# Borders between the stages of a two-layer sparse graph attention kernel: smaller units at two ends, an earlier mean row, buffers kept for the last stage

## The chip, the cores and the metric

The kernel runs on one core of one Trainium2 chip. The metric is the device time of that core in microseconds (us), lower is better. The time shown for the kernel before is the median of three runs. A profiled execution of the same kernel is shown beside it; all durations of single instructions come from that one.

## What is computed

Two graph attention layers over 4096 nodes with 512 features each. `adj` is a 4096 x 4096 matrix of 0 and 1, in which row n has few ones (its neighbours) except for the first rows. Cut to what matters:

```python
def _L0_gnn_ref(node_matrix, adj, W, a):          # 8 heads of 64
    h = einsum('nf,kfp->knp', node_matrix, W)
    e = leaky_relu(f2[:, :, None] + f1[:, None, :], 0.2)   # f1, f2: h times the halves of a
    att = softmax(where(adj[None] > 0, e, NEG_INF))
    return einsum('knm,kmp->knp', att, h)         # heads side by side: 512 features

def _L1_gnn_ref(x, adj, W1, a1, Wo, ao, lin1_w, lin1_b, lin2_w, lin2_b):
    x1 = elu(gat_heads(x, adj > 0, W1, a1))       # 8 heads of 64
    out = elu(gat_heads(x1, adj > 0, Wo, ao))     # 1 head of 512
    out = relu(out @ lin1_w + lin1_b)             # 1024 wide
    return out @ lin2_w + lin2_b

x = layernorm(x + _L0_gnn_ref(x, adj, ...))
x = layernorm(x + _L1_gnn_ref(x, adj, ...))
```

A node without neighbours gets, by the softmax over equal values, the mean of all rows of h. All arithmetic is in float32.

## The kernel before

There are three attention steps, called t0 (layer 0), t1 (the first attention of layer 1) and t2 (its second attention, with the two dense products behind it). In the text they are "layer 0", "layer 1" and "the last stage". Ahead of them one stage reads `adj` in 32 tiles of 128 rows and turns it into lists of edges (`find_edges`), with the projection for t0 beside it.

**Tables and gathers.** For each step a table in DRAM (`table_t0`, `table_t1`, `table_t2`) holds one row per node: its projected features and one or two scores. Row 4096, the last, is the mean of all rows; nodes without neighbours point at it. The edges of a tile of 128 nodes lie in chunks of 128 edges. One indirect DMA (line 1076), issued on the GpSimd queue (POOL), fetches the 128 table rows of a chunk into a slot of a buffer `g` with room for 6 chunks. A gather waits for every write to its table, the mean row among them.

**Units.** A tile's chunks are handled in units of up to 6 chunks (`units_of`). Each has two groups of slots, for the first and the second 64 nodes of the tile. There are 309 chunks and 66 units in each step. For every unit the loop runs, in this order on the engines:

- `weights` of the *next* unit: scores of the edges on VectorE (DVE, lines 1147 to 1150), their exponentials on ScalarE (ACT, lines 1152 to 1158). They wait for that unit's gathers.
- `add` of this unit: DVE writes selection matrices `sm` (line 1179, or 1187 in the last stage) and, in the two layers, scales the gathered rows (line 1200); TensorE (PE) sums them into `acc` (line 1212), 64 output rows at a time.
- the gather of the unit that takes over this unit's buffer: 7 ahead in the layers (`GB = 7`), 4 ahead in the last stage (`GT = 4`).

Between them stand the steps of a finished tile (`divide`, `norm`, `project`, `rows`, `split`), which make the next step's table: transposes (line 683), projection (line 697), the row `hrow` and its DMA to the table (line 711), and for every eight tiles `split_s`, five DVE instructions (lines 723 to 733) that cut the scores s into three bfloat16 parts. `spread` (lines 1101 to 1129) brings these scores to the edges of a tile with matmuls and two or more DVE instructions.

**The end of a layer.** Tile 0 is the last one, and has most edges; its last unit has 5 chunks, 5 slots in the first group and 1 in the second. In front of the last unit's `add`, `mean_of_all_but` makes the mean row's first part, out of all tiles but the last one (four DVE instructions, 16 matmuls and two ACT copies). When the last tile has been projected, `split` runs, then `rows`, and after everything `finish_mean` adds the last tile's part (lines 768 and 769) and sends the mean row (line 770). In the last round the split of s, which the DVE runs in order, comes ahead of the adds of `finish_mean`.

**The last stage.** At the end of the layers their memory is released. The last stage takes 4 buffers `g` of its own (pool `tg`), clears them on POOL (line 1428, four memsets), gathers for the first four units, and loads the weights of the dense products on the SyncE queue (SP): `sl1w` and `sl2w`, 2 MB each, then the biases. Buffers are cleared once because a slot that stands for no edge is not written by its gather, and what lies there must be a finite number. Layer 0 clears its 7 buffers the same way, on ACT (line 1288); layer 1 uses them on. The bias of the first dense product is loaded as 8 rows (`sl1b_r`) and turned with one transpose (line 1507) ahead of the first unit. Dense products are called in pieces between units (lines 1479 and 1491), at a pace set by the number of chunks.

All orders inside the layers and the last stage are written out by hand (`tc.manual_schedule()`); waits follow from the tiles and their pools. Where a pool lies in memory decides for whom its first writer waits: with `reuse_waits="tile"` a new tile waits for the last users of the tiles that lay at its place.

Of the kernel before, what the change touches and what calls it, by code (L numbers as in the profile page):

```python
# [10 lines left out]
F32 = mybir.dt.float32  # L11
# [10 lines left out]
P = 128  # L22
N = 4096
F = 512
NT = N // P
# [7 lines left out]
HC = HID // P  # L33
# [4 lines left out]
HS = 8  # L38
DM = 64
HN = P // 2  # L40
GC = 6
GB = 7
# [3 lines left out]
GT = 4  # L46
# [512 lines left out]
def sparse_path(  # L559
# [23 lines left out]
    nc = tc.nc  # L583
# [15 lines left out]
    ident = const.tile([P, P], F32, name="s_ident")  # L599
# [40 lines left out]
    st2 = Stage2("t2", 1, 512, dest_first=True)  # L640
# [391 lines left out]
    class Unit:  # L1032
# [3 lines left out]
        def __init__(self, t, runs, slots):  # L1036
# [2 lines left out]
            self.n = len(self.chunks)  # L1039
            self.first = self.last = False  # L1040

        def pick(self, a, base=0):

            at = 0
            for first, n in self.runs:
                yield slice(at, at + n), a[:, first - base : first - base + n]
                at += n
# [17 lines left out]
    class Attention:  # L1065
# [5 lines left out]

        def gather(self, u):

            u.g = self.gp.tile([P, GC, F + HS], F32, name="g")
            for k, c in enumerate(u.chunks):
                nc.gpsimd.indirect_dma_start(  # L1076
                    out=u.g[:, k, : self.st.row],
                    out_offset=None,
                    in_=self.st.table[:, :],
                    in_offset=bass.IndirectOffsetOnAxis(ap=idx[:, c : c + 1], axis=0),  # L1080
                    bounds_check=N,
                    oob_is_err=False,
                )
# [76 lines left out]
        def add(self, u):  # L1160

            hs, n = self.st.heads, u.n
# [8 lines left out]
            todo, at = [], 0  # L1171
            for g, slots in enumerate(u.slots):
                of_g = iota_n[:, g * HN : (g + 1) * HN]
                if hs > 1:
                    k, n_ = slots[0], len(slots)
                    c = u.chunks[k]
                    assert u.chunks[k : k + n_] == list(range(c, c + n_))
                    shape = [P, n_, HN]
                    nc.vector.tensor_tensor(  # L1179
                        sm[:, at : at + n_],  # L1180
                        of_g[:, None, :].to_broadcast(shape),
                        nl[:, c : c + n_, None].to_broadcast(shape),
                        op=OP.is_equal,
                    )
# [85 lines left out]
    def heads_layer(gp, wk, sb, pp, st, nxt, fetch, finish, clear):  # L1270
# [5 lines left out]
        order = [t for pair in zip(range(NT - 1, NT // 2, -1), many) for t in pair] + [NT // 2, 0]  # L1276
        assert sorted(order) == list(range(NT))
        units = units_of(order)
        with tc.tile_pool(name=f"ha_{st.name}", bufs=2, space=PSUM, reuse_waits="tile") as pacc, \
                tc.tile_pool(name=f"hp_{st.name}", bufs=1, space=PSUM, reuse_waits="tile") as one, \  # L1280
                tc.tile_pool(name=f"hq_{st.name}", bufs=2, space=PSUM, reuse_waits="tile") as ps, \
# [2 lines left out]
            extra = {}  # L1284
            if clear:
                for _ in range(GB):
                    g = gp.tile([P, GC * (F + HS)], F32, name="g")
                    nc.scalar.activation(g, ones.to_broadcast(g.shape), AF.Copy, scale=0.0)
            for u in units[:GB]:
                at.gather(u)  # L1290
# [38 lines left out]
            for i, u in enumerate(units):  # L1329
# [5 lines left out]
                run(project)  # L1335
                if i + 1 < len(units):
                    at.weights(units[i + 1])
                if i == len(units) - 1:
                    mrow = mean_of_all_but(pp, ps, nxt, u.t)
                at.add(u)  # L1340
                if i + GB < len(units):
# [8 lines left out]
                    spread()  # L1350
            ways.append((divide, order[-1]))
            while ways:
                for of in (project, split, rows, norm, divide):
                    run(of)
            finish_mean(ps, nxt, mrow)


    layers = ctx.enter_context(ExitStack())
# [24 lines left out]
        project_mean(sb, pp, st0)  # L1383


    wk = ctx.enter_context(tc.tile_pool(name="lw", bufs=3, reuse_waits="tile"))
    sb = ctx.enter_context(tc.tile_pool(name="ls", bufs=2, reuse_waits="tile"))
    pp = layers.enter_context(tc.tile_pool(name="lp", bufs=2, side="right", reuse_waits="tile"))
    gp = layers.enter_context(tc.tile_pool(name="lg", bufs=GB, side="right", reuse_waits="tile"))

    def fetch0(t):
        xr = sb.tile([P, F], F32, name="xr", bufs=3)
# [15 lines left out]


    layers.close()  # L1410
    with tc.tile_pool(name="tg", bufs=GT, side="right", reuse_waits="tile") as gp, \
            tc.tile_pool(name="tb", bufs=1, side="right", reuse_waits="tile") as big, \
            tc.tile_pool(name="ta", bufs=2, space=PSUM, reuse_waits="tile") as pacc, \
            tc.tile_pool(name="tp", bufs=1, space=PSUM, reuse_waits="tile") as ps, tc.manual_schedule():

# [7 lines left out]
        assert sorted(sum(blocks, [])) == list(range(NT))  # L1423
        order = [t for block in blocks for t in block]
        units = units_of(order)
        at = Attention(st2, gp, wk, pacc, ps)
        for _ in range(GT):
            nc.gpsimd.memset(gp.tile([P, GC, F + HS], F32, name="g"), 0.0)
        for u in units[:GT]:
            at.gather(u)  # L1430
        l1w = big.tile([P, FC, HID], F32, name="sl1w")
        nc.sync.dma_start(l1w, lin1_w.rearrange("(c p) o -> p c o", p=P))
        l2w = big.tile([P, HC, F], F32, name="sl2w")
        nc.sync.dma_start(l2w, lin2_w.rearrange("(c p) o -> p c o", p=P))
        l1b_r = big.tile([HC, P], F32, name="sl1b_r")
        nc.sync.dma_start(l1b_r, lin1_b.rearrange("(c p) -> c p", p=P))
        l2b = big.tile([P, F], F32, name="sl2b")
        nc.sync.dma_start(l2b, lin2_b.partition_broadcast(P))
        hts, hids, ready, open_ = {}, {}, [], []
# [63 lines left out]
            at.spread(t)()  # L1503
        at.weights(units[0])
        l1b = big.tile([P, HC], F32, name="sl1b")
        pb = ps.tile([P, HC], F32, name="pt")
        nc.tensor.transpose(pb, l1b_r, ident[:HC, :HC])
        nc.vector.tensor_copy(l1b, pb)


        pace = {t: 0.0 for t in blocks[0]}
# [2 lines left out]
            pace.update((t, 2 * len(last) / chunks) for t in block)  # L1514
        due, folded = 0.0, None
        for i, u in enumerate(units):
            pos = order.index(u.t)
            spread = at.spread(order[pos + 2]) if u.first and pos + 2 < NT else None
            if folded:
# [81 lines left out]
```

## Time and profile before

| | us |
|---|---|
| time before, median of 3 runs | 2330.81 (2325.15 to 2334.34) |
| profiled execution | 2138.83 |
| its span, first to last instruction | 2136.3 |
| PE busy in the span | 1721.8 (81%) |
| DVE busy | 1328.6 (62%) |
| POOL busy | 1162.0 (54%) |
| ACT busy | 663.4 (31%) |
| mean granted PE clock of the profiled execution | 0.918 |

The profiled execution is 9% shorter than the runs without a profile; sums are made against its own time. Layer 0 begins to gather at 500.5 us, layer 1 at 944.1 us and the last stage at 1384.2 us. A line of the timeline gives start and duration in us, engine, line of the kernel, operation, what it writes and reads, how many were merged, and in brackets the idle time before it with what ended it.

### The profile page before, as it was taken

Reading aid. Unit: us, or ns where it says so; the run is one execution under the profiler, and the core shown is the slowest. Engines: PE = TensorE matmul, PEld = TensorE weight load, DVE = VectorE, ACT = ScalarE, POOL = GpSimd, SP = SyncE. Lnnn points to the kernel's source line nnn. Section 1 sums busy time; section 2 is a strip of 40 time slices with the busy share of each in tenths; the row PEclk is TensorE's granted clock in tenths of the full one; section 3 lists DMA queues with packets and bytes.
Section 4 is the critical chain, followed back from the end, with each engine's and each line's share of the span. In section 5 each row is a group of like instructions: output and inputs, shape, how many; then the busy total and the mean of one; then the engine's idle time right before and its main releaser. Section 6 shows DMA issues by size and latency. Waiting matters only on the chain.

```text
span 2136.3 us, 29277 instructions
## 1 busy us (share of the span) xinstructions
PE 1721.8 (81%) x8987; PEld 1004.8 (47%) x8987; DVE 1328.6 (62%) x3920; ACT 663.4 (31%) x2311; POOL 1162.0 (54%) x1662
## 2 busy tenths in 40 slices
PE   4878777663798888857887888569999998998997
PEld 3655443221465565534555655344444444444444
DVE  5787777774889998837878878433434343433413
ACT  3346777664222232102333332111110212111121
POOL 5514444346777777727777777473547443543200
PEclk8999998786999999878999999889999999999999
DMA  6434566544777878727767776463546343534301
GB/s 229 132 109 168 188 250 238 201 153 130 228 233 231 248 242 243 208 67 191 196 185 195 195 198 190 151 165 102 156 119 177 113 128 96 148 103 120 96 19 46
DMA packets 132589, 351.94 MB, mean 165 GB/s; under 512 B 41922, under 2 KB 42954, under 8 KB 128454
## 3 DMA queue, kind: packets, MB, share of 16 engines
q0 software_dynamic: 74160, 206.25, 35.4%
q1 hardware_dynamic: 58262, 143.72, 19.1%
q8 instruction: 74, 1.21, 0.2%
q14 instruction: 93, 0.76, 0.1%
HBM read 347.31 MB, written 42.24 MB: 182 GB/s over the span
## 4 chain that ended last, share of the span: by engine, by line
PE 33%; DVE 17%; issue 16%; POOL 15%; DMA 12%; ACT 6%; SPq 0%; POOLq 0%; DVEq 0%; ACTq 0%
POOL g L1076 10%; DMA g<-table_t,idx 10%; PE acc L1212 10%; PE p L1479 9%; PE ph L697 6%; DVE g L1200 4%; PE p L1491 4%; DVE cand L884 2%; POOL s L944 1%; ACT sides L943 1%; DMA xr<-sx_d 1%; DVE cand L901 1%; DVE sm L1179 1%; DVE lst L899 1%; PE pl L967 1%
## 5 line engine op out<-in xcount | busy, mean ns | idle before, releaser
L1076 POOL DMA_INDIRECT g<-table_t,idx x927 | 937.8, 1012 | 535.9 <-issue 229.1
L1212 PE MATMUL acc<-g,sm 128*64 128x260 f32 (+2 forms) x4068 | 581.0, 416 | 182.7 <-DVE g L1200 141.6
L1212 PEld LDWEIGHTS acc<-g,sm 128*64 128x64 f32 x4068 | 327.9, 148 | 402.1 <-DVE g L1200 159.5
L697 PE MATMUL ph<-sw_t,xt 128*128 128x264 f32 (+1 forms) x1536 | 399.5, 409 | 54.3 <-ACT xt L686 47.8
L697 PEld LDWEIGHTS ph<-sw_t,xt 128*128 128x128 f32 x1536 | 296.5, 199 | 126.3 <-ACT xt L686 70.6
L1200 DVE TENSOR_TENSOR g<-g,wp 128x2048 f32<-128x2048 f32 (+3 forms) x132 | 348.9, 2644 | 3.4 <-ACT wp L1155 3.4
L884 DVE MAX8 cand<-key 128x8 f32<-128x353 f32 (+55 forms) x467 | 196.3, 446 | 77.6 <-PE key L878 76.8
L1479 PE MATMUL p<-sht,sl1w 128*128 128x512 f32 (+1 forms) x576 | 228.9, 553 | 0.5 <-DVE xr L1496 0.5
L1491 PE MATMUL p<-sl2w,shid 128*128 128x512 f32 x512 | 226.7, 597 | 0.0
L686 ACT ACTIVATE xt<-pt 128x128 f32<-128x128 f32 x384 | 101.1, 278 | 214.3 <-PE pt L683 213.9
L1479 PEld LDWEIGHTS p<-sht,sl1w 128*128 128x128 f32 x576 | 108.0, 191 | 111.6 <-issue 106.0
L1491 PEld LDWEIGHTS p<-sl2w,shid 128*128 128x128 f32 x512 | 95.2, 190 | 119.8 <-issue 119.4
L1147 DVE TENSOR_TENSOR z<-s,g 128x16 f32<-128x16 f32 (+8 forms) x291 | 46.6, 175 | 162.7 <-DMA g<-table_t,idx 161.6
L877 PE MATMUL key<-sg,s_identb 128*128 128x512 bf16 (+1 forms) x258 | 111.5, 433 | 14.3 <-DVE cand L884 9.0
L1482 ACT ACTIVATE shid<-p,sl1b 128x512 f32<-128x512 f32 (+1 forms) x72 | 46.0, 639 | 242.8 <-PE p L1479 242.8
L1249 DVE SCALAR_TENSOR_TENSOR o<-ex,o 128x512 f32<-128x512 f32 x64 | 44.2, 691 | 122.0 <-ACT ex L1248 121.8
L848 ACT ACTIVATE sg<-raw 128x4096 bf16<-128x4096 int32 (+1 forms) x39 | 116.9, 2998 | 6.3 <-DMA raw<-in_adj_dram 3.4
L710 ACT COPY hrow<-ph 128x260 f32<-128x260 f32 (+2 forms) x194 | 70.5, 372 | 152.3 <-PE ph L697 152.0
L878 PE MATMUL key<-frac,places 128*128 128x512 bf16 (+1 forms) x258 | 111.4, 433 | 2.7 <-POOL places L784 2.7
L1187 DVE TENSOR_SCALAR sm<-iota_n,nl,w 128x64 f32<-128x64 f32 x339 | 83.6, 327 | 31.2 <-ACT w L1158 31.2
L1155 ACT ACTIVATE wp<-z 128x32 f32<-128x32 f32 (+3 forms) x132 | 27.2, 206 | 211.2 <-DVE g L1200 211.2
L1496 DVE TENSOR_TENSOR xr<-p,xr 128x512 f32<-128x512 f32 x32 | 22.0, 689 | 93.6 <-PE p L1491 93.2
(185 smaller groups left out, 1853.5 us busy)
## 6 DMA issues: line engine op xcount, KB each, us to landing
raw<-in_adj_dram SPq DMA_DIRECT2D x31, 2048.0 KB, 7.7
table_t<-hrow SPq DMA_DIRECT2D x64, 260.0 KB, 3.2
xr<-in_x_dram SPq DMA_DIRECT2D x64, 256.0 KB, 3.9
g<-table_t,idx POOLq DMA_INDIRECT x927, 3.8
table_t<-hrow SPq DMA_DIRECT2D x32, 257.0 KB, 4.4
sx_d<-o SPq DMA_DIRECT2D x32, 256.0 KB, 4.0
xr<-sx_d SPq DMA_DIRECT2D x32, 256.0 KB, 4.4
out_dram<-xr SPq DMA_DIRECT2D x32, 256.0 KB, 2.3
```

Source lines behind the costliest of these rows:

```text
L686: nc.scalar.activation(xt[:, c, :], pt[:, c, :], AF.Copy, accum_out=st.xparts[:, c, t : t + 1])
L697: nc.tensor.matmul(ph[:n], columns(c), st.w[:, c, j], start=(c == 0), stop=(c == FC - 1))
L848: nc.scalar.activation(sg[:, ts(i, w)], raw[:, ts(i, w)], AF.Sign)
L877: nc.tensor.matmul(out_, ident_b, sg[:, j:e], start=True, stop=False)
L878: nc.tensor.matmul(out_, places[:, w], frac[:, j - w * KW : e - w * KW], start=False, stop=True)
L884: nc.vector.max(out=cand[:, at : at + 8], in_=part)
L1076: nc.gpsimd.indirect_dma_start(out=u.g[:, k, : self.st.row], out_offset=None, in_=self.st.table[:, :], in_offset=bass.IndirectOffsetOnAxis ...
L1187: nc.vector.tensor_scalar(sm[:, at + i], of_g, node[k], u.w[:, k], op0=OP.is_equal, op1=OP.mult)
L1200: nc.vector.tensor_mul(body, body, wp[:, :, :, None].to_broadcast(body.shape))
L1212: nc.tensor.matmul(out_[g * HN : (g + 1) * HN], sm[:, slot], rows(k), start=start, stop=stop)
L1479: nc.tensor.matmul(p1, l1w[:, c, ts(k, P)], hts[b][:, c, :n], start=(c == 0), stop=(c == FC - 1))
L1491: nc.tensor.matmul(p2, hids[b][:, k, ts(j, P)], l2w[:, k, :], start=(k == 0), stop=(k == HC - 1))
```

## The change

Four edits:

1. The last unit of each layer is cut in two: all chunks but the last two, and the last two (`Unit.cut`). The first unit of the last stage is cut into its first two chunks and the rest.
2. `mean_of_all_but` is called one unit of tile 0 earlier (two units ahead of the last, counted with the cut).
3. In the last rounds of a layer `rows` runs ahead of `split`, and `finish_mean` directly behind the last `rows`.
4. Four of the layers' seven buffers `g` lie in a pool `lk` that is kept; the last stage goes on with these four and doesn't clear any. The four memsets on POOL go. Buffers are handed out by a counter: turns 0 to 3 of every 7 from the kept pool, 4 to 6 from the pool `lg`, which ends with the layers. In the last stage `sl1b_r` is loaded ahead of the weights, and its transpose and copy come at the third unit.

```diff
+        def cut(self, m):
+            (first, n), = self.runs
+            one = Unit(self.t, [(first, m)], [[k for k in slots if k < m] for slots in self.slots])
+            two = Unit(self.t, [(first + m, n - m)], [[k - m for k in slots if k >= m] for slots in self.slots])
+            one.first, two.last = self.first, self.last
+            return [one, two]
...
-            u.g = self.gp.tile([P, GC, F + HS], F32, name="g")
+            u.g = self.gp()
...
-                if hs > 1:
+                if hs > 1 and slots:
...
         units = units_of(order)
+        units[-1:] = units[-1].cut(units[-1].n - 2)
...
-                    g = gp.tile([P, GC * (F + HS)], F32, name="g")
+                    g = gp().rearrange("p k f -> p (k f)")
                     nc.scalar.activation(g, ones.to_broadcast(g.shape), AF.Copy, scale=0.0)
...
-                if i == len(units) - 1:
+                if i == len(units) - 3:
                     mrow = mean_of_all_but(pp, ps, nxt, u.t)
...
             while ways:
-                for of in (project, split, rows, norm, divide):
+                for of in (project, rows, split, norm, divide):
                     run(of)
-            finish_mean(ps, nxt, mrow)
+                    if of is rows and len(out_) == NT:
+                        finish_mean(ps, nxt, mrow)
...
+    keep = ctx.enter_context(tc.tile_pool(name="lk", bufs=GT, reuse_waits="tile"))
     wk = ctx.enter_context(tc.tile_pool(name="lw", bufs=3, reuse_waits="tile"))
...
-    gp = layers.enter_context(tc.tile_pool(name="lg", bufs=GB, side="right", reuse_waits="tile"))
+    more = layers.enter_context(tc.tile_pool(name="lg", bufs=GB - GT, side="right", reuse_waits="tile"))
+    turns = [0]
+    def gp():
+        turns[0] += 1
+        return (keep if (turns[0] - 1) % GB < GT else more).tile([P, GC, F + HS], F32, name="g")
...
-    with tc.tile_pool(name="tg", bufs=GT, side="right", reuse_waits="tile") as gp, \
-            tc.tile_pool(name="tb", bufs=1, side="right", reuse_waits="tile") as big, \
+    with tc.tile_pool(name="tb", bufs=1, side="right", reuse_waits="tile") as big, \
...
-        at = Attention(st2, gp, wk, pacc, ps)
-        for _ in range(GT):
-            nc.gpsimd.memset(gp.tile([P, GC, F + HS], F32, name="g"), 0.0)
+        units[:1] = units[0].cut(2)
+        at = Attention(st2, lambda: keep.tile([P, GC, F + HS], F32, name="g"), wk, pacc, ps)
         for u in units[:GT]:
             at.gather(u)
+        l1b_r = big.tile([HC, P], F32, name="sl1b_r")
+        nc.sync.dma_start(l1b_r, lin1_b.rearrange("(c p) -> c p", p=P))
         l1w = big.tile([P, FC, HID], F32, name="sl1w")
...
-        l1b_r = big.tile([HC, P], F32, name="sl1b_r")
-        nc.sync.dma_start(l1b_r, lin1_b.rearrange("(c p) -> c p", p=P))
...
-        pb = ps.tile([P, HC], F32, name="pt")
-        nc.tensor.transpose(pb, l1b_r, ident[:HC, :HC])
-        nc.vector.tensor_copy(l1b, pb)
...
         for i, u in enumerate(units):
+            if i == 2:
+                pb = ps.tile([P, HC], F32, name="pt")
+                nc.tensor.transpose(pb, l1b_r, ident[:HC, :HC])
+                nc.vector.tensor_copy(l1b, pb)
             pos = order.index(u.t)
```

## The prediction

> **What bounds the kernel now.** I read the page's chain of waits first, then the windows of the stretch between layer 1 and the last stage, then its timeline, because every edit sits at a border between stages: the end of layer 0 (near 920 us), the end of layer 1 (near 1360 us), the start of the last stage (near 1384 us).
>
> ```profile
> PE 33%; DVE 17%; issue 16%; POOL 15%; DMA 12%; ACT 6%; SPq 0%; POOLq 0%; DVEq 0%; ACTq 0%
> ...
> 1370.00:1380.00 10.00, 5.13 (x29) 3.27 (x27) 4.05 (x11) 0.81 (x3) 4.04 (x2) 0.84 0.12 43
> 1380.00:1390.00 10.00, 0.00 (x0) 0.00 (x0) 0.00 (x0) 0.00 (x0) 8.62 (x7) 0.50 0.37 105
> 1390.00:1400.00 10.00, 0.00 (x0) 0.00 (x0) 0.87 (x6) 0.21 (x1) 7.56 (x9) 0.50 0.64 179
> ...
> 1440.00:1450.00 10.00, 10.00 (x65) 7.76 (x64) 3.56 (x15) 3.73 (x8) 7.56 (x9) 1.00 0.73 194
> ```
>
> No one engine owns the chain, so a change pays only where its stage waits. The windows (length, then busy PE, weight load, DVE, ACT, POOL, then clock, DMA share, GB/s) show such a place: from 1380 to 1400 TensorE does nothing, and from about 1427 it is full. The timeline says why.
>
> ```profile
> 1350.34 2.70 POOL L1428 MEMSET g<- 128x3120 f32 x1 [1.35 <-PE acc L1212]
> ...
> 1373.26 2.70 POOL L1428 MEMSET g<- 128x3120 f32 x1 [20.22 <-PE ph L697]
> ...
> 1373.66 1.03 PE L768 MATMUL ph<-hrow,s_share 128*1 128x256 f32 x4 [0.46 <-ACT ss_t L717]
> ...
> 1373.92 2.07 DVE L730 CAST s_t<-s 128x16 bf16<-128x16 f32 x1
> ...
> 1376.56 0.73 DVE L769 TENSOR_TENSOR mrow<-mrow,ph 1x256 f32<-1x256 f32 x2
> ...
> 1377.32 0.25 SPq L770 DMA_DIRECT2D table_t<-mrow  x1
> ...
> 1378.65 5.34 POOL L1428 MEMSET g<- 128x3120 f32 x2 [2.70 <-DMA table_t<-mrow]
> ...
> 1384.15 1.00 POOL L1076 DMA_INDIRECT g<-table_t,idx  x1 [0.16 <-POOL g L1428]
> ...
> 1422.57 0.17 DVE L1147 TENSOR_TENSOR z<-s,g 128x6 f32<-128x6 f32 x1 [3.43 <-DMA g<-table_t,idx]
> ...
> 1423.68 3.35 PE L1212 MATMUL acc<-g,sm 128*64 128x257 f32 x24 [2.85 <-DVE sm L1187]
> ...
> 1426.97 7.17 PE L1479 MATMUL p<-sht,sl1w 128*128 128x256 f32 x32
> ```
>
> The reader is to see one chain: the last row of the table is projected, the mean row's second part waits on DVE behind the split of s (whose CAST takes 2.07 us, while the same CAST took 0.18 at 1321.94), the mean row is sent at 1377.32, two memsets follow on POOL, and only then the first gather goes at 1384.15. After that the gathers pace everything, one per 1.3 us on POOL, until the 27th chunk: it lands by 1422.57, lets the sums of the tile before it start at 1423.68, and from 1426.97, the first dense product, TensorE has no gap. So what counts is when chunk 27 lands. Last, the tail of both layers:
>
> ```profile
> 910.65 8.45 PE L1212 MATMUL acc<-g,sm 128*64 128x260 f32 x56 [0.71 <-DVE g L1200]
> 919.03 3.72 PE L697 MATMUL ph<-sw_t,rest_mean 128*1 128x264 f32 x16
> 922.68 4.60 PE L1212 MATMUL acc<-g,sm 128*64 128x260 f32 x24
> ...
> 1344.12 7.92 PE L1212 MATMUL acc<-g,sm 128*64 128x260 f32 x40 [3.40 <-DVE g L1200]
> 1353.54 1.97 PE L1212 MATMUL acc<-g,sm 128*64 128x260 f32 x16 [1.51 <-DVE g L1200]
> 1355.44 3.63 PE L697 MATMUL ph<-sw_t,rest_mean 128*1 128x257 f32 x16
> 1359.00 4.60 PE L1212 MATMUL acc<-g,sm 128*64 128x260 f32 x24
> ```
>
> In layer 0 TensorE runs without a gap from 910.65 to 927.28; in layer 1 there is one of 1.51 us ahead of 1353.54.
>
> **What the Trainium skill says.** "SBUF — State Buffer", section "SBUF: two separate sides": DVE and GpSimd share a port pair, which one instruction holds to its end while the other stands still. The trace agrees: the CAST that began at 1373.92 ended at 1375.99, with the memset (1373.26 + 2.70 = 1375.96). "DMA: Bandwidth & Descriptors", section "Queues, rings and completion order": each DMA engine takes turns between the queues that have work, packet by packet. No stretch of this trace shows a large load against gathers, so that is the open cost below. The same page, section "Anatomy of one DMA": most of a small transfer's fixed time is the receipt of its last write. The trace agrees: the mean row of layer 0 was issued at 942.13 and the gather it releases started at 944.12, 1.99 us later, for 2 KB.
>
> **The change part by part.**
>
> *The tail of a layer.* The last unit (5 chunks) becomes 3 and 2, and the mean row's first part (16 matmuls, 3.6 to 3.7 us) goes ahead of the unit before them. TensorE's work is the same: the 24 sums of the last unit lie almost all in one half of the columns and take 4.60 us (other units of 24, with both halves filled, take 2.78), cut or not. In layer 0 TensorE has no gap to lose: gain 0. In layer 1 DVE waited until 1350.21 for the fifth chunk, since the next unit's weights stand ahead of this unit's scaling. With three chunks to wait for (1345.39 issued, landing by about 1348.9 with the 3.7 us of its neighbours) scaling of the unit ends near 1352.8, and the mean's matmuls, ready near 1350.2, fill the gap from 1352.04. Then 3.63 + 1.97 + 4.60 from 1352.04 ends at 1362.2 instead of 1363.6: 1.4 us. The extra unit costs DVE some five instructions of 0.2 to 0.5 us and ACT two, beside TensorE's 10 us: nothing on the path.
>
> *finish_mean ahead of the split.* Layer 0: the two adds ended at 942.11; without five split instructions in front they follow the matmuls (939.93 + 1.04 = 940.97) and end at 941.4: 0.7 us. The last hrow, data moved by 941.6, with the 1.3 us from the mean row's data (942.8) to its release, is done by 942.9, before the new 943.4, so it does not take the wait over. Layer 1: adds end at 1373.66 + 1.03 + 0.4 = 1375.1, issue 1375.17 instead of 1377.32: 2.15 us, the CAST's stall in it (no memset is left to hold the port). The five split instructions (0.9 us) go behind the adds; the scores they feed are not wanted before the first gather lands, 9 us later.
>
> *No clearing in the last stage.* The first gather then follows the mean row by 2.0 us as in layer 0, not by 1384.15 - 1377.32 = 6.83: 4.83 us. Sum at this border: 1.4 + 2.15 + 4.83 = 8.4, first gather near 1375.75.
>
> *What the kept buffers move.* Built programs show the weights' new places and queue order. sl1w and sl2w (2 MB each) lay on buffers that came free at 1352 and 1355, stood on SP ahead of the last hrow, and moved while nothing was gathered:
>
> ```profile
> q1 hardware_dynamic: 1568, 4.19, 57.6%
> ```
>
> That is 1350 to 1370. Now they lie on the other three buffers, read by layer 1's last units, and SP has them behind the hrow and the mean row: issue near 1374.5, data from about 1375.4. At the 400 GB/s they had, 4.2 MB takes 10.5 to 11.2 us, now under the gathers, whose data start near 1377.3. Bounds: nothing, if the gathers pass first; 11.2 us, if they stand behind. In between, packet by packet: some 1350 load packets are left at 1377.3, each with one 2 KB row of a gather beside it. That is 3.4 MB at 400 GB/s (8.6 us) and 2.8 MB at the 265 GB/s that gathers reach per full share (133 GB/s at 50%, in 1384 to 1392), 10.5 us: 19 us for 10.5 gathers, where POOL issues 14.6. Four are late, five with the l2b and xr loads behind. Then a gather takes 0.99 us of the engines against 1.3 of POOL, so the backlog of 5 shrinks by 0.24 per us. Chunk 27 is issued near 1411.6, 15 us after 1396: 1.3 are left, 1.3 us late. I take a loss of 1.3; the ends are 0 and, if POOL cannot run ahead of the backlog, about 6.
>
> *The first unit cut to 2 and 3, l1b's transpose put to the third unit.* TensorE starts 5 chunks earlier with a third of its work for that tile, but the later units still wait for their chunks: 0. The four buffers now hold 15 chunks, not 21, at the start; the fifth unit's gather needs the first unit's sums, done before POOL is there (15 x 1.3 = 19.5 us on). The transpose and its copy (0.27 and 0.16 us) lie in a gap of some 3 us.
>
> *Start of layer 0.* The cleared buffers now lie on edge tables; the first clear waits for the last read of iota_k (496.43 + 0.28), not for ACT alone (496.56): at most 0.25 us lost.
>
> Sum: 8.4 + 0.7 - 0.25 - 1.3 = 7.5 us. The profiled execution took 2138.8 us (span 2136.3), so about 2131. The timed runs stand at 2330.8, with a lower clock presumably (none is shown for them); the border's time is POOL, DVE and DMA latency, so I carry 7.5 us over as it is: 2323, 0.3% below.
>
> **The rivals.** (a) Full gain and more: the loads do not disturb, and in timed runs a slower TensorE is itself the bound of the first units and gains from the earlier first sums (at chunk 5 rather than 10, up to 6 us). For it: the cut; against: gathers pace until 1423. 8.9 + 4 to 6 = 13 to 15, 2317. (b) The gain is swallowed: the backlog also holds POOL, which stays about 6 us late at chunk 27, or timed runs have no gap at 1353: 0 to 3 us left, 2329. (c) Slower: the weight loads take the gathers' place. If gathers stand behind the 11.2 us of loads, l2b and xr (another 1.5 to 2), and POOL stops with them, chunk 27 is 13 us late against 9 gained: +4, 2335. It decides once the loads cost more than 8.9 us. For it: in the profile these loads share no window with the gathers; against: turns packet by packet, and POOL's even 1.3 us in all layers under 190 to 250 GB/s.
>
> **How the numbers follow.** Forecast 0.58, (a) 0.17, (b) 0.15, (c) 0.10. What this kernel's measurement can tell from no change is 0.5%, 11.7 us here; only (a) passes it surely, and its neighbours in part: faster 0.2. Slower by more needs (c) three times over, or a cost I do not see: 0.1. Same 0.7. The forecast's own range is 2320 to 2326 by the bounds of the loads; the spread of the three runs (2325 to 2334) comes on top, and half of each outer case: 2312 to 2333.
>
> **What would show it.** The first last-stage gather near 1375.8 with the earlier span unchanged but for 0.7 us at 944; no memset at this line; the CAST at 0.18 us; sl1w's transfer between 1375 and 1396 with gathers landing later than 3.7 us after issue; the first dense product near 1419.5, and every later mark 7 to 8 us early. Wrong would be: gathers that start after 1378 (another wait took over), POOL gaps over 0.3 us before chunk 27, or a first dense product not moved.

## The result, and the profile after

| | us |
|---|---|
| before, beside the changed kernel (20 runs) | 2334.49 (2321.84 to 2350.53) |
| after (20 runs) | 2322.12 (2312.11 to 2338.45) |
| ratio | 0.9957, 95% interval 0.9939 to 0.9975 |
| the changed kernel measured once more (7 runs, k9 below) | ratio 0.9942, 0.992 to 0.9963 |

Pooled by the width of their intervals the two measurements give 0.9951 ± 0.0014, that is 11.4 ± 3.2 us less. The forecast was 7.5 us, at 2323 us.

The profile shown of before (the first profile, below) has a span 8% under the timed runs, 2136.3 us at a mean granted clock of 0.918, while all later profiles, like the timed runs, show 2307 to 2355 us at 0.874 to 0.891; after (2336.3 us, 0.879) is therefore compared with a second profile of the kernel before, k0 (2345.0 us, 0.882). This is the chain of waits of k0, by engine:

```profile
PE 44%; DVE 15%; issue 14%; POOL 7%; another core or an unknown queue 7%; ACT 7%; DMA 5%; SPq 0%; POOLq 0%; DVEq 0%; ACTq 0%
```

and this the same line of after:

```profile
PE 46%; DVE 16%; issue 13%; ACT 7%; another core or an unknown queue 7%; POOL 6%; DMA 4%; SPq 0%; DVEq 0%; POOLq 0%; ACTq 0%
```

The item "another core or an unknown queue" does not stand in the chain of the first profile. The program has one core, so these 7% (about 164 us in either) are waits whose cause the trace does not show. One such place lies 36 us after the first gather of the last stage in k0 ("remote" is the timeline's word for the same item, "issue" means that the engine waited for nothing that the trace shows; rows between are left out):

```profile
1611.70 0.17 DVE L1224 RECIPROCAL rd<-acc 128x1 f32<-128x1 f32 x1 [5.65 <-remote]
...
1611.94 1.01 POOL L1076 DMA_INDIRECT g<-table_t,idx  x1 [1.18 <-remote]
...
1612.14 6.04 PE L1212 MATMUL acc<-g,sm 128*64 128x257 f32 x24 [9.19 <-issue]
...
1616.68 0.58 ACT L1457 COPY sht<-pt 128x512 f32<-128x512 f32 x1 [15.33 <-remote]
```

TensorE stands for 9.19 us, VectorE and POOL go on within half a microsecond of it, and ScalarE's copy of four transposes, recorded as done at 1602.96, starts only at 1616.68. In the first profile the same 24 sums start 30.9 us after the first gather, in k0 36.7 us. What holds TensorE there, no run settles.

The border between layer 1 and the last stage, in the timeline of after (start and duration in us, engine, line, operation, in brackets the idle time before it and what ended it; rows between are left out):

```profile
1562.96 0.32 SPq L711 DMA_DIRECT2D table_t<-hrow  x1
...
1562.98 1.03 PE L768 MATMUL ph<-hrow,s_share 128*1 128x256 f32 x4 [0.46 <-ACT ss_t L717]
1563.61 0.84 DVE L769 TENSOR_TENSOR mrow<-mrow,ph 1x256 f32<-1x256 f32 x2 [7.75 <-PE ph L768]
...
1564.49 0.24 SPq L770 DMA_DIRECT2D table_t<-mrow  x1
1564.59 0.18 DVE L730 CAST s_t<-s 128x16 bf16<-128x16 f32 x1
...
1565.78 0.40 SPq L1450 DMA_DIRECT2D sl1w<-in_lin_w_dram  x1
1566.41 0.40 SPq L1452 DMA_DIRECT2D sl2w<-in_lin_w_dram  x1
...
1566.96 1.00 POOL L1084 DMA_INDIRECT g<-table_t,idx  x1 [31.87 <-DMA table_t<-hrow]
```

From the last row of the table sent (hrow) to the first gather it is now 4.00 us; in k0 it is 10.51 and in the profile shown of before 10.52. The mean row goes 1.53 us after the hrow instead of 3.69, the CAST takes 0.18 us instead of 2.07, and no memset stands between the mean row and the gather. The two large weight loads now leave just ahead of the first gather.

The windows from the last hrow on show what these loads do (length, busy PE, weight load, DVE, ACT, POOL, then granted clock, DMA share, GB/s). First k0, in the stretches hrow to first gather, the next 24 us, and on to the first dense product:

```profile
1564.90:1575.40 10.50, 1.93 (x17) 0.95 (x17) 4.05 (x11) 0.09 (x2) 7.71 (x3) 0.75 0.21 76
1575.40:1599.40 24.00, 6.95 (x34) 4.52 (x36) 4.75 (x26) 0.62 (x3) 18.45 (x19) 0.54 0.61 162
1599.40:1626.30 26.90, 14.60 (x85) 7.79 (x81) 8.77 (x32) 5.05 (x10) 18.92 (x19) 0.75 0.51 133
```

and after in the same three:

```profile
1562.90:1567.00 4.10, 1.70 (x16) 0.76 (x16) 1.88 (x11) 0.09 (x2) 0.04 (x1) 1.00 0.26 80
1567.00:1591.00 24.00, 8.40 (x23) 4.48 (x24) 3.18 (x17) 0.61 (x3) 18.52 (x19) 0.52 0.99 357
1591.00:1617.00 26.00, 16.37 (x95) 8.46 (x93) 10.08 (x40) 4.05 (x10) 17.70 (x19) 0.79 0.49 132
```

The first stretch shrank from 10.5 to 4.0 us. In the second, the DMA engines are full (share 0.99, 357 GB/s) where they were at 0.61; POOL issues its 19 gathers in 24 us in both. The third ends at the first dense product, about as long after the first gather as in k0 (50.05 against 50.79 us).

### The profile page after: what moved, and what is told of

Read it like the earlier page. It is cut to its first block, busy times and chain, and to the rows that moved or that the text cites. A ratio compares the mean times of both kernels' runs of the same rounds, so it can differ in the third digit from the quotient of the medians.

```text
span 2336.3 us, 29301 instructions
## 1 busy us (share of the span) xinstructions
PE 1771.7 (76%) x8987; PEld 1040.1 (45%) x8987; DVE 1331.3 (57%) x3933; ACT 660.7 (28%) x2316; POOL 1151.6 (49%) x1658
## 4 chain that ended last, share of the span: by engine, by line
PE 46%; DVE 16%; issue 13%; ACT 7%; another core or an unknown queue 7%; POOL 6%; DMA 4%; SPq 0%; DVEq 0%; POOLq 0%; ACTq 0%
PE acc L1220 15%; PE ph L697 11%; PE p L1495 10%; PE p L1507 5%; DVE g L1208 3%; POOL g L1084 2%; DMA xr<-sx_d 2%; DVE cand L884 2%; DMA g<-table_t,idx 2%; PE pt L683 1%; POOL s L944 1%; DVE cand L901 1%; DVE lst L899 1%; ACT sides L943 1%
## 5 line engine op out<-in xcount | busy, mean ns | idle before, releaser
L1220 PE MATMUL acc<-g,sm 128*64 128x260 f32 (+2 forms) x4068 | 587.9, 414 | 175.3 <-DVE g L1208 91.7
L697 PE MATMUL ph<-sw_t,xt 128*128 128x264 f32 (+1 forms) x1536 | 436.4, 437 | 146.5 <-ACT xt L686 80.6
L1220 PEld LDWEIGHTS acc<-g,sm 128*64 128x64 f32 x4068 | 332.9, 146 | 395.1 <-issue 123.9
L697 PEld LDWEIGHTS ph<-sw_t,xt 128*128 128x128 f32 x1536 | 323.0, 217 | 229.2 <-ACT xt L686 97.9
L1208 DVE TENSOR_TENSOR g<-g,wp 128x2048 f32<-128x2048 f32 (+4 forms) x134 | 349.3, 2607 | 37.9 <-ACT wp L1163 18.7
L1155 DVE TENSOR_TENSOR z<-s,g 128x16 f32<-128x16 f32 (+9 forms) x294 | 44.7, 174 | 82.9 <-DMA g<-table_t,idx 81.2
L686 ACT ACTIVATION_READ_ACCUMULATOR xt<-pt 128x1 f32 x384 | 79.9, 208 | 0.0
L1228 DVE RECIPROCAL rd<-acc 128x8 f32<-128x8 f32 x64 | 13.1, 205 | 114.4 <-PE acc L1220 73.3
```

The costliest lines, as they stand in the source:

```text
L686: nc.scalar.activation(xt[:, c, :], pt[:, c, :], AF.Copy, accum_out=st.xparts[:, c, t : t + 1])
L697: nc.tensor.matmul(ph[:n], columns(c), st.w[:, c, j], start=(c == 0), stop=(c == FC - 1))
L1208: nc.vector.tensor_mul(body, body, wp[:, :, :, None].to_broadcast(body.shape))
L1220: nc.tensor.matmul(out_[g * HN : (g + 1) * HN], sm[:, slot], rows(k), start=start, stop=stop)
```

## The experiments

Ratios are to the kernel before on the same chip, with the 95% interval. "Hrow to gather" is the time from the issue of the last hrow of layer 1 to the first gather of the last stage. "Chunk 10" is the time from the first gather of the last stage to the weights that need its tenth chunk; "dense" the time from that gather to the first dense product.

| | ratio | hrow to gather | chunk 10 | dense |
|---|---|---|---|---|
| k0 before again | 0.9997 (0.9975 to 1.0019) | 10.51 | 15.65 | 50.79 |
| k1 edit 4's buffers only | 0.9975 (0.9957 to 0.9993) | 3.83 | 20.05 | 53.19 |
| k2 edit 3 only | 0.9999 (0.9977 to 1.0022) | 8.62 | 15.54 | 51.38 |
| k6 both of these, no cuts | 0.9986 (0.9959 to 1.0012) | 3.87 | 19.70 | 52.45 |
| k3 edits 1 and 2 in the layers only | 0.9997 (0.9969 to 1.0025) | 10.52 | 15.48 | 52.29 |
| after | 0.9957 (0.9939 to 0.9975) | 4.00 | 18.33 | 50.05 |
| k9 after again | 0.9942 (0.992 to 0.9963) | 3.83 | 18.39 | 50.51 |
| k4 after, loads ahead of the gathers | 0.997 (0.9949 to 0.999) | 3.56 | 15.53 | 49.93 |
| k5 after, bias ahead of the first unit | 0.9952 (0.9935 to 0.9969) | 3.50 | 18.59 | 48.53 |
| k10 k5 again | 0.9961 (0.9941 to 0.9982) | 3.92 | 18.27 | 52.66 |
| k7 k5 with the first unit whole | 0.9975 (0.9955 to 0.9995) | 3.53 | 18.49 | 52.93 |
| k11 k7 again | 0.9957 (0.994 to 0.9974) | 3.77 | 18.25 | 53.14 |
| k8 k5 without the cuts in the layers | 0.9971 (0.9956 to 0.9986) | 3.65 | 18.46 | 53.13 |

**k0: the kernel before, profiled and timed against itself.**

> The kernel before once more, so that its trace is taken in an execution as long as the timed ones. Ratio 1.000 within 0.002. Theory (latency at the border): from the last hrow's issue to the last stage's first gather 10.5 us as in the first profile, whatever the clock; from the first gather to the first dense product 42.8 us if gathers pace this stretch. Rival (a slower TensorE paces it in timed runs): that second interval is near 50 us, as in the profile of the changed kernel (50.1).

Ratio 0.9997: differences below 0.2% are not told apart here. Hrow to gather is 10.51 us as in the first profile, but the first dense product comes at 50.79 us, as the rival had it, and not at 42.8. The reason that the rival gave, a slower TensorE, is a part of it at most: the granted clock was 0.54 and 0.75 in the two stretches up to there, but TensorE also stood 9.19 us for no recorded reason.

**k1, k2, k6: the border edits, one by one and together.** k1 has only the kept buffers (the counter that hands them out is as in the change):

```diff
+    keep = ctx.enter_context(tc.tile_pool(name="lk", bufs=GT, reuse_waits="tile"))
...
-        for _ in range(GT):
-            nc.gpsimd.memset(gp.tile([P, GC, F + HS], F32, name="g"), 0.0)
```

> Only the kept buffers (no memsets in the last stage), no cut, no earlier mean, split still ahead of finish_mean. Theory: the CAST takes 0.18 us instead of 2.07 and the gather follows the mean row by 2.0 to 2.5 us instead of 6.8: hrow to first gather 10.5 - 1.9 - 4.5 = about 4.2 us, ratio 0.997 (6 of 2331 us). Rival (the gain of 10 us comes from the cut units and the earlier mean): ratio 0.999 to 1.000, since what is won at the border is lost in the stretch behind it to the weight loads.

k2 has only the other order of the last steps:

```diff
-                for of in (project, split, rows, norm, divide):
+                for of in (project, rows, split, norm, divide):
                     run(of)
-            finish_mean(ps, nxt, mrow)
+                    if of is rows and len(out_) == NT:
+                        finish_mean(ps, nxt, mrow)
```

> Only finish_mean ahead of the split. Theory: 0.7 us at the end of layer 0; at the end of layer 1 the adds no longer stand behind the CAST that the memset holds: mean row 2.1 us sooner, the two memsets and the gather with it, hrow to first gather 8.4 us; in all 2.8 us, ratio 0.9988. Rival (the memsets behind it hide it, or the hrow's landing takes over): hrow to first gather stays at 10 or more, ratio 1.000.

k6 has both:

> The kernel before with edit 3 and the kept buffers of edit 4, no unit cut, the mean row's first part where it was, the bias where it was. Theory: the two border edits overlap (either removes the CAST's stall), hrow to first gather 4.0 us instead of 10.5 and 0.7 us at the end of layer 0, so 7.2 us, ratio 0.9969 (0.995 to 0.999). Rival: the changed kernel's time needs the cuts, and this one stands with the kept buffers alone, ratio 0.9975 or above, its first dense product 2 to 3 us later after the first gather (53 instead of 50) because sums start only at the fifth chunk.

The steps come out as worked out, and they overlap. Without the memsets (k1) the CAST takes 0.18 us although it still stands ahead of the mean row, and hrow to mean row falls from 3.69 to 1.81 us. With the other order alone (k2) the mean row goes after 1.53 us, but the first gather follows it by 7.09 us where k0 has 6.82, so 1.9 us is left of 2.2. Together the step is 3.9 us, no shorter than in k1. The time agrees with that: k1 and k6 pooled are 0.9978 ± 0.0015, 5.0 ± 3.5 us. k2 alone cannot be told from nothing, and k6 alone, 0.9986, lies nearer to what its rival expected, though its interval holds the expected 0.9969 too. At the end of layer 0, hrow to first gather fell from 4.26 to 3.58 us in k2 and to 3.6 in every version with that edit: 0.7 us.

k1 and k6 pay something that the changed kernel doesn't: their bias is still loaded behind the weights, which now move with the gathers, and still turned ahead of the first unit. VectorE waits 7.5 and 6.4 us for it, and the weights of chunk 10 follow at 20.05 and 19.70 us for that reason. Their first dense product comes 2 to 3 us later than in after, as the rival of k6 had it, but the whole first unit cannot be the reason alone: k8 and k10, where that unit is cut, show 53.13 and 52.66 us.

**k3, k8: the tail of the layers.** k3 is the kernel before with the cut of each layer's last unit and the earlier first part of the mean row:

```diff
...
+        units[-1:] = units[-1].cut(units[-1].n - 2)
...
-                if i == len(units) - 1:
+                if i == len(units) - 3:
                     mrow = mean_of_all_but(pp, ps, nxt, u.t)
```

> The kernel before with edits 1 and 2 in the two layers only: the last unit of a layer cut in two, the first part of the mean row one unit of tile 0 earlier. Theory (my prediction): nothing at the end of layer 0, 1.4 us at the end of layer 1, so 1.4 us in all, ratio 0.9994 (0.998 to 1.001 by the spread of the measurement); the step from the last hrow to the first gather stays at 10.5 us, the CAST at about 2.07 us. Rival: the cuts carry what the border edits left of the changed kernel's 12 us, 4 us or more, ratio 0.998 or less, and TensorE reaches the last hrow several us earlier in both layers. Second rival: two more instructions per engine at the end of each layer cost something, ratio above 1.001.

k8 is k5 with these same lines taken back.

> The changed kernel with the bias ahead of the first unit and the layers' last units whole, the mean row's first part where it was before. Theory: the cut at the end of the two layers is worth 1.4 us at the second (my prediction) or about 1.7 us at each (from the marks of the nine runs so far: 50.3 against 48.6 us and 48.7 against 47.0 us from the 12th last gather to the last hrow), so 1.4 to 3.4 us or 0.06 to 0.15% slower than the version with the bias first, and marks near 50.3 and 48.7. Rival: the cuts are worth nothing, marks of 48.6 and 47.0 here too, no difference of time.

The times are too coarse alone: 0.7 ± 6.5 us for k3, and k8 stands 0.0015 ± 0.002 behind k5 and k10 pooled (0.9956 ± 0.0013), 3.5 ± 4.6 us. The traces say more. I took the time from the twelfth-last gather of a layer, which belongs to a unit that the cut leaves alone, to the last hrow, in every profile but the first. At the end of layer 0 it is 50.6 us on average without the cuts (k0, k1, k2, k6, k8: 49.8 to 51.5) and 49.1 with them (eight profiles, 47.6 to 51.1): 1.5 ± 1.0 us. At the end of layer 1 it is 48.9 (47.5 to 49.7) and 46.9 (45.6 to 47.4): 2.0 ± 1.1 us. k8, the last to run, lies with the versions without cuts at both ends (51.5 and 49.7).

What the cuts changed in TensorE's work can be seen in its last 80 sums and the 16 matmuls of the mean between them. Without the cuts, at the end of layer 1 in k1:

```profile
1521.72 8.45 PE L1212 MATMUL acc<-g,sm 128*64 128x260 f32 x56 [2.06 <-DVE g L1200]
1530.10 3.63 PE L697 MATMUL ph<-sw_t,rest_mean 128*1 128x257 f32 x16
1533.65 4.60 PE L1212 MATMUL acc<-g,sm 128*64 128x260 f32 x24
```

and with them, in after:

```profile
1536.65 6.35 PE L1220 MATMUL acc<-g,sm 128*64 128x260 f32 x40 [0.64 <-DVE g L1208]
1542.94 3.63 PE L697 MATMUL ph<-sw_t,rest_mean 128*1 128x257 f32 x16
1546.50 6.35 PE L1220 MATMUL acc<-g,sm 128*64 128x260 f32 x40
```

From the first to the last line that is 16.53 and 16.20 us, so the cut saves about 0.3 us. The same holds at the end of layer 0, where all versions without the cuts take 16.6 us and all with them 16.3. Two profiles show much longer rows there, one of either kernel: the 56 sums took 9.77 us in k0, and 40 sums took 8.04 us in k9, which is the changed kernel. In both the granted clock was low.

```profile
1535.93 9.77 PE L1212 MATMUL acc<-g,sm 128*64 128x260 f32 x56 [2.37 <-DVE g L1200]
...
1538.30 8.04 PE L1220 MATMUL acc<-g,sm 128*64 128x260 f32 x40 [2.52 <-DVE g L1208]
```

The windows of these two and of the 40 sums of after, in this order, end in clock, DMA share and GB/s:

```profile
1535.93:1545.70 9.77, 9.77 (x57) 6.15 (x58) 9.56 (x21) 1.17 (x6) 2.70 (x1) 0.83 0.10 11
1538.30:1546.34 8.04, 8.04 (x41) 4.82 (x42) 7.76 (x23) 1.14 (x6) 0.00 (x0) 0.79 0.00 0
1536.65:1543.00 6.35, 6.34 (x41) 4.07 (x42) 6.14 (x18) 0.84 (x4) 0.00 (x0) 1.00 0.00 0
```

The rest of the 1.5 and 2.0 us is not in these matmuls. Most of it lies ahead of them, where TensorE's mean clock, taken from the twelfth-last gather to the last sum, was 0.91 to 0.96 without the cuts and 0.91 to 1.00 with them. No run separates the cuts from the clock there.

**k4: the weight loads taken out of the gathers' way.** The two loads go through POOL's queue ahead of the gathers, and the buffers of the pool `lg` are used three units earlier so that they come free sooner:

```diff
-        return (keep if (turns[0] - 1) % GB < GT else more).tile([P, GC, F + HS], F32, name="g")
+        return (keep if (turns[0] + 2) % GB < GT else more).tile([P, GC, F + HS], F32, name="g")
...
+        nc.gpsimd.dma_start(l1w, lin1_w.rearrange("(c p) o -> p c o", p=P))
...
+        nc.gpsimd.dma_start(l2w, lin2_w.rearrange("(c p) o -> p c o", p=P))
         for u in units[:GT]:
             at.gather(u)
...
-        nc.sync.dma_start(l1w, lin1_w.rearrange("(c p) o -> p c o", p=P))
...
-        nc.sync.dma_start(l2w, lin2_w.rearrange("(c p) o -> p c o", p=P))
```

> The changed kernel, but the 4 MB of dense weights lie on buffers that come free three units sooner and are sent on POOL's queue behind layer 1's last gather, so that they move before the last stage's gathers. Theory (the loads cost the gathers 1 to 3 us, made up by chunk 15 to 27): the tenth chunk is ready 15.5 us after the first gather instead of 18.3, ratio to the kernel before 0.995 to 0.9955, at most 3 us better than the changed kernel. Rival (the loads take most of the gain): 0.992 or less, 5 us or more better than the changed kernel.

The gathers are undisturbed again: chunk 10 at 15.53 us as in the kernel before, against 18.33 in after. So the collision is real and delays these weights by 2.8 us. But the delay is gone further on: the weights that need the 27th chunk come at 42.2 us in k4 and 42.4 in after, where VectorE no longer waits for a gather in either, and the first dense product at 49.9 and 50.1. The time is no better: k4 stands 4.4 ± 5.8 us behind the changed kernel. That result is open in part, since sending the loads from POOL may have a cost of its own.

**k5, k10: a new wait, and what it costs.** In after, VectorE's copy of the turned bias (the first dense product's) stands ahead of the weights of a unit and waits for a transpose that TensorE has behind the sums of the unit before. VectorE's timeline of after:

```profile
1593.36 0.17 DVE L1533 COPY sl1b<-pt 128x8 f32<-128x8 f32 x1 [6.60 <-PE pss L1116]
1593.57 0.17 DVE L1155 TENSOR_TENSOR z<-s,g 128x5 f32<-128x5 f32 x1
```

k5 and k10 put transpose and copy back ahead of the first unit:

```diff
         l1b = big.tile([P, HC], F32, name="sl1b")
+        pb = ps.tile([P, HC], F32, name="pt")
+        nc.tensor.transpose(pb, l1b_r, ident[:HC, :HC])
+        nc.vector.tensor_copy(l1b, pb)
...
-            if i == 2:
-                pb = ps.tile([P, HC], F32, name="pt")
-                nc.tensor.transpose(pb, l1b_r, ident[:HC, :HC])
-                nc.vector.tensor_copy(l1b, pb)
```

> The changed kernel with the transpose of the bias and its copy back ahead of the first unit of the last stage. In the changed kernel the copy, ahead of the weights of the 15th chunk, stood 6.60 us on VectorE for a transpose that TensorE had behind the sums of the second unit. Theory: this wait is off the path, since TensorE is busy to the 27th chunk anyway; the weights of the 15th chunk come some 3 us after the first gather earlier (22 to 24 us instead of 26.6), the first dense product at 49 to 50 us after the first gather as before, ratio to the kernel before 0.9957 as the changed kernel. Rival: the wait holds the chain of weights and sums to the first dense product, which comes 2 to 6 us earlier, ratio 0.994.

> The changed kernel with the bias turned ahead of the first unit, once more. Theory: the wait of 6.6 us was off the path, so the same time as the changed kernel beside it, within 0.1%. Rival: 1 to 2 us faster than that, first dense product at 48.6 us as in its first run, and the best of all versions.

These weights then come 23.7 and 23.0 us after the first gather instead of 26.6 and 28.1 (after, k9), but the first dense product at 48.5 in one and 52.7 in the other, and the time is the same: 0.9956 ± 0.0013 against 0.9951 ± 0.0014. So a wait of 6.6 us on VectorE cost nothing that these runs can measure. The two profiles of this one program also show what the mark "dense" is worth. POOL waits 2.67 us before the 22nd gather in k10 and 0.76 us in k5. In all six profiles with the first product at 52.4 us or later and the kept buffers (k1, k6, k7, k8, k10, k11) POOL waits 2.3 to 2.8 us there, and in after, k9 and k4 it does not. The trace does not name what POOL waits for.

**k7, k11: the first unit of the last stage whole.** They are k5 with this line of the change taken back:

```diff
-        units[:1] = units[0].cut(2)
```

> The changed kernel with the first unit of the last stage whole, and the bias ahead of the first unit as in the kernel before. Theory (my prediction): the cut of the first unit is worth nothing, first sums at 16 to 19 us after the first gather instead of 12.4, but the first dense product at 50 to 51 us as in the changed kernel, ratio 0.9957 to 0.996. Rival: where TensorE is slower the first sums set the pace, and without the cut the first dense product comes 2 to 4 us later, ratio 0.997.

> The changed kernel with the bias ahead of the first unit and the first unit of the last stage whole, once more. In its first run its first dense product came at 52.9 us after the first gather, against 48.6 with the unit cut, and its ratio was 0.9975 against 0.9952. Theory now: the cut is worth 3 to 4 us, so about 0.15% slower than the version above and first dense product at 52 to 53 us. Rival (my prediction): the cut is worth nothing, both the same within 0.1%, and the first pair of ratios was chance.

The two runs, 0.9975 and 0.9957, pooled 0.9965 ± 0.0013, stand 0.0009 ± 0.0018 behind k5 and k10, 2.1 ± 4.3 us: no gain is shown, and one of 4 us is not excluded. The trace says why little can come of the cut. TensorE's first sums in after, where the first gather is at 1566.96:

```profile
1579.38 3.68 PE L1220 MATMUL acc<-g,sm 128*64 128x257 f32 x8 [13.73 <-DVE sm L1195]
1586.28 5.47 PE L1220 MATMUL acc<-g,sm 128*64 128x257 f32 x16 [3.22 <-DVE sm L1195]
```

and in k7, where it is at 1566.71:

```profile
1586.05 6.06 PE L1220 MATMUL acc<-g,sm 128*64 128x257 f32 x24 [19.17 <-DMA g<-table_t,idx]
```

With the cut the sums begin 12.4 us after the first gather instead of 19.3, but the 24 sums end at 24.8 us instead of 25.4: of 6.9 us head start 0.6 are left. The reason is in VectorE's order: the weights of the next unit, which need chunk 10, stand ahead of the selection matrices `sm` of the cut unit's second part, as they do for the whole unit in k7 (18.49 us after the first gather there, 18.33 in after):

```profile
1585.28 0.17 DVE L1155 TENSOR_TENSOR z<-s,g 128x5 f32<-128x5 f32 x1 [5.36 <-DMA g<-table_t,idx]
...
1585.77 0.99 DVE L1195 TENSOR_SCALAR sm<-iota_n,nl,w 128x64 f32<-128x64 f32 x4
```

From there on the sums run at half clock in both, nearly to their end.

**k9: the changed kernel beside the last three.**

> The changed kernel once more, beside the next three on the same chip, since differences of 0.2% are at stake. All theories: 0.9957 to the kernel before, 0.994 to 0.9975. Its profile says how far the marks repeat: 12th last gather of a layer to the last hrow about 49 and 47 us (end of layer 0, of layer 1), last hrow to first gather 4.0 us, first dense product 50 us after the first gather.

The marks repeat: 50.5 us to the first dense product (50.05 in after), 3.83 us from hrow to gather.

## Why the prediction was right, step by step

The forecast of about 0.3% less held, and the two steps at the borders did as it said. That the time itself came out at 2322 us for 2323 is partly luck. The kernel before had a median of 2334.5 us beside it, not 2330.8, and the pooled gain of 11.4 ± 3.2 us leaves the forecast's 7.5 just outside. The term of the tail was too small, and two steps (the gap at the end of layer 1, and chunk 27 as the pace) rest on the first profile alone: the later ones do not show them.

- *Border edits (forecast 6.98 us from hrow to gather).* Right: 6.5 us in after, 6.6 to 7.0 in the other versions with the kept buffers, of 10.5. The mean row's part was exact (2.16 for 2.15 us). The part of the memsets came to 4.4 of 4.83 us in after, because there the trace names the last hrow and not the mean row as what released POOL, 4.0 us after its issue. In k5 it names the mean row, 1.97 us after its issue, as forecast. The prediction had worked out which of the two lands last for layer 0, and not for this border.
- *End of layer 0, finish_mean (0.7 us).* Right: 4.26 to 3.58 us.
- *The tail of the layers (0 at layer 0, 1.4 us at layer 1).* This term was mis-sized: the marks give 1.5 ± 1.0 and 2.0 ± 1.1 us, 3.5 ± 1.5 for 1.4. The mechanism described for layer 1 is not what the later profiles show. It was a gap of 1.51 us between the 40 and the 16 sums, which the mean's matmuls would fill; in all five versions without the cuts these 56 sums run as one row, with no gap to fill. So 1.4 us against 2.0 there is a likeness of numbers. At layer 0 "TensorE has no gap to lose" was right as a reading of the row, but a gain of 0 did not follow: with the cuts the same sums take 0.3 us less. Where the rest comes from stays open at both ends.
- *Weight loads under the gathers (a loss of 1.3 us).* That the two share the DMA engines was right. The Trainium skill, "DMA: Bandwidth & Descriptors", section "Queues, rings and completion order", says that an engine takes turns between its queues packet by packet. The trace agrees in that neither stood: in the 20 us after the first gather the loads' queue moved 4.57 MB in 1785 packets and the gathers' queue 2.85 MB in 1013. It does not show the single turns. Chunk 10 was 2.8 us late and at chunk 27 VectorE no longer waited for a gather. What is left of this at the end is not resolved: k4 against after shows no cost, and the first dense product moves by more than 1.3 us between two profiles of one program.
- *Chunk 27 sets the pace ("what counts is when chunk 27 lands").* True of the first profile, where VectorE waited 3.43 us for that gather. In k0 VectorE has been idle for 0.11 us when it turns to these weights, 44.2 us after the first gather, with the 27th gather issued at 34.3 us. TensorE's unexplained stand of 9.19 us lies before them. The gain at the border was carried over all the same, because what follows took as long as before.
- *The first unit cut (0).* Not contradicted: 2.1 ± 4.3 us. The reason given, that the later units still wait for their chunks, fits: the second part of the first unit already stands behind chunk 10. Rival (a) foresaw the slower TensorE, but its 4 to 6 us do not follow, because the head start is used up within that unit.
- *The bias at the third unit ("lies in a gap").* It did not lie in a gap: it made VectorE wait 6.60 us. It cost nothing that k5 and k10 could measure.
- *Start of layer 0 (0.25 us).* Not resolved: the first clear is at 496.6 and 497.5 us in the two profiles of before, and anywhere from 494.4 to 499.2 in those with the kept buffers.
- *The first dense product, 7 to 8 us earlier.* From the last hrow it comes 54.1 us later in after and 54.3 in k9, against 61.3 in k0, 60.0 in k2 and 62.8 in k3: about 7 us. The other versions with the kept buffers lie between 52.0 and 57.0, and k5 and k10, one program, are 4.5 us apart, so single profiles do not fix this mark.

Summed as measured: 6.5 + 0.7 + 3.5 = 10.7 us, less what the loads cost, against 11.4 ± 3.2 us in the timed runs. Of these, 7.2 us are traced to their instructions; of the 3.5 ± 1.5 only 0.7 are. From the first gather of the last stage to the end, the profiles with the kept buffers took 766.6 to 775.2 us (after 769.3, k9 768.2) and those without 767.7 to 769.6: nothing measurable was gained or lost behind the border, in agreement with where the forecast put its gain.

Rival (b), the gain swallowed, falls with k1 and after, although its doubt about the gap at 1353 was right. Rival (c), the loads in the gathers' place and the kernel slower, falls with the time and with chunk 27. Rival (a), 13 to 15 us, lies in part inside the measured interval. It was right about the clock, but the gain it expected behind the first gather is not there.

## What to carry to other kernels

Between two stages with a barrier of data, take the chain from the last producer to the first consumer apart instruction by instruction: what is queued ahead on each engine without being needed (a split, a clear) can be worth its full length, and after each removal ask again what lands last. Weight loads that moved under the next stage's gathers cost nothing measurable here, where the gathers with two small loads had kept the DMA engines 0.61 busy: look for such room first. And before two profiles are compared, set their spans, granted clocks and chains side by side: if these differ, profile the old kernel again, measure from marks inside the stage, and read the clock of a row before calling it slow for another reason.

## What was unexpected of the hardware

- TensorE works at half clock for long at the start of the last stage: the mean granted clock was 0.52 to 0.54 over the first 24 us in k0 and after. 24 sums took 6.06 us there (k7), and 3.35 in the profile shown of before at a clock of 1.00 (at 1423.68). The Trainium skill, "TensorE: Matmul & The Clock Gate", section "What's actually happening", says that the clock is halved after an idle window of about 3.4 us and restored after a busy one. The trace agrees: after 13.7 us without work the clock was 0.50. In after it came back only as the second burst of 5.5 us ended at 1591.75, so that it was full during the wait behind it and half again in the next sums. Sums made earlier in two bursts were thus made no faster there. In k5, with the same cut, it came back as the first burst ended, and the second took 4.25 us.
- Two 2 MB loads and a stream of gathers together reached 357 GB/s over 24 us (after). In k0, where these loads had moved earlier, the same 19 gathers with two small loads made 162 GB/s, at POOL's 1.3 us per gather.

The clock's return and loss in after (clock, DMA share and GB/s are the last three numbers):

```profile
1589.00:1592.00 3.00, 3.00 (x12) 1.42 (x10) 0.00 (x0) 0.00 (x0) 2.24 (x3) 0.55 0.55 178
1592.00:1595.00 3.00, 0.61 (x6) 0.19 (x2) 1.53 (x9) 0.21 (x1) 2.39 (x3) 1.00 0.37 98
1595.00:1598.00 3.00, 2.71 (x13) 1.47 (x14) 1.64 (x5) 1.26 (x2) 2.37 (x3) 0.52 0.70 182
```
